# A four-layer graph network in one core: a planner that stays in a division of the array, and what is computed and loaded at the start

## The chip, the core and the metric

The kernel runs on one core of a Trainium2 chip. A core has five engines that run side by side, each with its own queue in program order: TensorE (matmuls, into PSUM), VectorE, ScalarE, GpSimd (POOL) and SyncE (SP), which here issues all DMAs. They wait for each other through semaphores. The metric is the time of one execution on the device in microseconds, as the median of several runs. The profiler's span, from the first to the last instruction, is a little shorter.

TensorE's array has 128 rows and 128 columns. It can be used whole (128\*128 in the profile), or divided: into four quarters of 64\*64, or into two halves of 128\*64. The text calls these ways of use divisions.

## The reference

All is float32. There are 128 graphs of 64 nodes with 512 features. Four layers are applied, each with a sum with its input and a layer norm over the features. Cut to what matters:

```python
# layer 0
y = x @ w;  s = y @ a
A = s[..., :, None] + s[..., None, :]
A = jnp.tanh(A / 8.0) * 8.0;  A = jnp.where(A >= 0, A, 0.1 * A)
A = jnp.exp(A) * adj;  A = A / A.sum(-1) * adj.sum(-1)      # keepdims
x = ln(x + A @ x @ w)
# layer 1
q, k, v = x @ Wq.T + bq, x @ Wk.T + bk, x @ Wv.T + bv
weight = adj * jnp.exp(q @ k.T)
x = ln(x + weight / weight.sum(2) @ v)
# layer 2
q, k = split(x @ Wqk);  v = x @ Wv
w = mask / sqrt(512) * (q * (adj @ (k * mask))).sum(-1)
x = ln(x + softmax(w)[:, :, None] * v)
# layer 3, two hypergraph convolutions; H = (adj != 0)
conv(x, W, b) = D^-1 H B^-1 H.T (x @ W.T) + b
h = ln(relu(conv(x, W1, b1)), gamma, beta)
x = ln(x + conv(h, W2, b2) + x)
```

Layer 1 needs Wq and Wk only as their product, Wq' Wk, and so does layer 2 with its two halves of Wqk. Layer 3 needs H B^-1 H' once for each graph. Its gamma can be multiplied into the rows of W2, and beta W2 is one row that is added.

## The kernel before, in words

The 8192 nodes are 64 tiles of 128 (two graphs each). A group is two tiles (GT), a chunk is two groups (GC); there are 32 groups and 16 chunks. The function `run` writes down the sixteen steps of one group, from layer 0 to the store of its output.

Large products are done by a seven-product scheme (`seven_products`): four blocks of the left side, four sums of them made on VectorE (`side_sums`), and for the weights seven pieces prepared once (`combine`), kept in DRAM and read again for every group (`streamed`, eight `ring` buffers of 512 KB). Small products per graph work in quarters: `e,x`, `gm,x` and `gm,h` (a graph's matrix times its features, in `gathered`), `e,same` (sums over a graph, `over_graph`), `ident,col`, `k,e` and `ones,e` (layer 1), and `ones,adj`, `w,kept` and `kept,kept` (a chunk's sums, and H B^-1 H'). The scores `k,k` work in column halves. All the rest takes the whole array. The profile names an instruction in this way, out<-in, by the buffers' names without numbers.

The order of all instructions on all engines is made when the program is built, by the class `Order`. Each operation is recorded by `order.add` with its engine, a cost in ns, the buffers that it reads and writes, a key (less is more urgent), and on TensorE a mode ("whole", "quarters" or "columns"). For each group `keys_by_what_follows` sets the keys from the longest chain behind an operation, between 0 and 16 steps past the group's own base (BASE). `run` of the class then plays the engines through with these costs: on each engine that is free it takes the most urgent operation that is ready and has its buffers. On TensorE, where the mode of the most urgent one differs from that of the last, an operation of the last mode is taken instead if it is within NEAR of it:

```python
if e == "SP" and heap[0][0] > far or found and heap[0][0] > found[0] + self.NEAR:
    break
```

A change of mode costs TURN ns in this play, a DMA costs 60 ns of SP and lands after its bytes have passed a link of BYTES_PER_NS, and 2200 ns. Every engine's instructions are then pinned in the order found. Since one function emits all, nearly every instruction has the same line in the profile (L1111 before).

The preparation touches these parts. `load_x`, `raw` and `load_adj` load the first group's x, the weights and the chunk's adj; w0 with its vector a0 comes first (key -11.5), x and adj after it, wq1 and wk1 at -10, wqk2 at 3. `gram` makes `m1` from wq1 and wk1, and `m2` from wqk2: four banks of four 128x512 matmuls each, copied by ScalarE. `emit_u1` makes Wk' bq by 16 matmuls of one column. `emit_bw` makes beta W2 by 16 matmuls of 128x256, and VectorE multiplies gamma into W2. `prepare_chunk` makes a chunk's H (`hA`), B^-1 (`bh`), masks and sums; H B^-1 H' (`emit_g`, buffer `gm`) is made in `run`, for each group. `normalized` does a layer norm for the two tiles of a group at once: statistics on VectorE, the power -1/2 on POOL, the scaling on ScalarE. PSUM has four buffers `bank` for single use and two pairs `chx`, `chz` for the seven products.

Of the kernel before, what the change touches and what calls it, by code (L numbers as in the profile page):

```python
# [13 lines left out]
ALU = mybir.AluOpType  # L14
# [44 lines left out]
class Order:  # L59
    LATENCY = {"PE": 220, "DVE": 70, "ACT": 60, "POOL": 60, "SP": 2200}  # L60
    BYTES_PER_NS = 230
    TURN = 100
    NEAR = 0.25
# [52 lines left out]
    def run(self):  # L116
# [5 lines left out]
        port_free, port_user = 0, None  # L122
# [5 lines left out]
        while len(done) < len(self.ops):  # L128
# [4 lines left out]
            for e, heap in ready.items():  # L133
                while free_at[e] <= now:
                    skipped, held, found = [], set(), None
                    while heap:
                        if e == "SP" and heap[0][0] > far or found and heap[0][0] > found[0] + self.NEAR:
                            break
                        item = heappop(heap)
                        need = defaultdict(int)  # L140
                        wants = [b for b in item[2].touches if b.slot is None]
                        for b in wants:
                            need[b.kind] += 1
                        if item[2].port and port_free > now:
                            skipped.append(item)
                        elif all(k not in held and len(self.slots[k]) >= c for k, c in need.items()):
                            fits = e != "PE" or item[2].mode == mode
                            if found is None or fits:
                                if found:
                                    skipped.append(found)  # L150
                                found, takes = item, wants
                            else:
                                skipped.append(item)
                            if fits or found[0] < 0:
                                break
                        else:
                            held.update(need)
                            skipped.append(item)
                    for item in skipped:
                        heappush(heap, item)  # L160
                    if found is None:
                        break
                    moved, found = True, found[2]
                    turn = 0
                    if e == "PE":
                        turn, mode = self.TURN if found.mode != mode else 0, found.mode
                    found.start = now
                    done.append(found)
                    found.takes = takes
                    for b in takes:  # L170
                        b.slot = self.slots[b.kind].pop()
                    end = free_at[e] = now + found.cost + turn
                    if found.port:
                        port_free = end
                        if e == "POOL":
                            found.behind = port_user
                        else:
                            port_user = found
                    if e == "SP":
                        link = max(link, now) + found.bytes // self.BYTES_PER_NS  # L180
                        end = max(end, link)
                    seen = end + self.LATENCY[e]
                    heappush(events, (free_at[e], n, None, None))
                    for u in found.users:
                        n += 1
                        heappush(events, (free_at[e] if u.engine == e and e != "SP" else seen, n, u, None))
                    for b in found.touches:
                        n += 1
                        heappush(events, (seen, n, None, b))
                    n += 1  # L190
# [34 lines left out]
def kernel(  # L225
# [46 lines left out]
    kind("gm", 3, GT, N)  # L272
# [29 lines left out]
    def dma(size, reads, writes, out, in_):  # L302
        order.add("SP", 60, reads, writes, lambda: nc.sync.dma_start(out=out(), in_=in_()), size=size)
# [61 lines left out]
    def raw(w, n, kind_="k4", first=()):  # L365
# [3 lines left out]
        for h in range(n):  # L369
            b = Buf(kind_, 2)  # L370
            order.add("SP", 60, [], [b, *(first if h == 0 else ())],
# [5 lines left out]
    def rows_of(b, cols):  # L377
        return b.t.rearrange("p (c o) -> p c o", o=cols)

    load_x(0)  # L380
# [4 lines left out]
        lambda: bass.AP(tensor=a0.tensor, offset=a0.offset, ap=[[0, P], [1, D]]))  # L385
    load_adj(0)
    mask_c = plain_in("mask_c", mask, T)
    order.key = -10.0
    wq1_raw, wk1_raw = raw(wq1, 2), raw(wk1, 2)
# [64 lines left out]
    def in_dram(which, width):  # L454
# [6 lines left out]
        def store(k, piece):  # L461
# [8 lines left out]
            order.add("SP", 60, [piece[0], in_turn], [dst[i % n]], emit, size=P * width * 4)  # L470
# [37 lines left out]
    def gram(name, left, right):  # L508
# [5 lines left out]
        def emit(ps, c):  # L514
            for k in range(KC):
                nc.tensor.matmul(ps.t, rows_of(left[k // 2], D)[:, k % 2, ts(c, P)], rows_of(right[k // 2], D)[:, k % 2],
                                 start=(k == 0), stop=(k == KC - 1))

        for c in range(KC):
            ps = Buf("bank")  # L520
            pe(w_pe(D, KC), left + right, [ps], lambda ps=ps, c=c: emit(ps, c))
# [11 lines left out]

    def emit_u1(ps):
        for c in range(KC):
            for k in range(KC):
                nc.tensor.matmul(ps.t[:, c : c + 1], rows_of(wk1_raw[k // 2], D)[:, k % 2, ts(c, P)], bq_c.t[:, k : k + 1],
                                 start=(k == 0), stop=(k == KC - 1))

    ps_u1 = Buf("bank")  # L540
    pe(w_pe(1, KC * KC), wk1_raw + [bq_c], [ps_u1], lambda: emit_u1(ps_u1))
# [3 lines left out]
    wqk_h = wqk2.rearrange("(h o) i -> h o i", h=2)  # L545
    order.key = 3.0
    wq2_raw, wk2_raw = raw(wqk_h[0], 2), raw(wqk_h[1], 2)
    order.key = 5.0
    m2 = gram("m2", wq2_raw, wk2_raw)

    order.key = 7.0
    stored_in_place("v2", quarter_views(raw(wv2, 2, first=[in_turn]), D), D, HALF)

    def quarters(w):
# [4 lines left out]
        for h in range(2):  # L559
            for i in range(2):  # L560
                q = Buf("k4")
                order.add("SP", 60, [in_turn] if made else [], [q] if made else [q, in_turn],
# [8 lines left out]
    order.key = 9.0  # L571
# [3 lines left out]
    ps_bw = Buf("bank")  # L575

    def emit_bw():
        for i in range(2):
            for c in range(KH):
                nc.tensor.matmul(ps_bw.t[:, ts(i, D // 2)], beta_c.t[:, c : c + 1].to_broadcast([P, P]),  # L580
                                 w3b_q[f"b{c // 4 + 1}{i + 1}"][1]()[:, c % 4, :], start=(c == 0), stop=(c == KH - 1))

    pe(w_pe(D // 2, 2 * KH), [beta_c] + [b[0] for b in w3b_q.values()], [ps_bw], emit_bw)
    act(D, [ps_bw], [bw_b], lambda: nc.scalar.activation(bw_b.t, ps_bw.t, AF.Identity, scale=0.5), NOW)
    for k, (q, view) in w3b_q.items():
        for c in range(KH // 2):
            row = (int(k[1]) - 1) * (KH // 2) + c
            dve(D // 2, [gamma_c, q], [q], lambda view=view, c=c, row=row: nc.vector.tensor_scalar(
                view()[:, c, :], view()[:, c, :], gamma_c.t[:, row : row + 1], None, ALU.mult))
    stored_in_place("3b", w3b_q, PIECE, PIECE)  # L590

    def streamed(which, room=()):
# [3 lines left out]
        for src, n in stored[which]:  # L596
            width = PIECE // src.cells
            t_ = Buf("ring")
            order.add("SP", 60, [src[list(range(n))]], [t_, *(room if not pieces else ())],
# [26 lines left out]
    def prepare_chunk(c):  # L626
        order.key = BASE[GC * c] - 3.0 if c else -9.0
# [42 lines left out]

        order.key += 6.0
# [7 lines left out]
        prepared[c] = adj, turned_adjs[c], hA, bh, am, radj, g1, dc, dh  # L679
# [164 lines left out]
    def normalized(reads_of, view, n_stats, eps, n):  # L844

        mv = Buf("col", GT)
        for t in range(GT):
# [4 lines left out]
            dve(12, [st], [mv[t]], lambda t=t, st=st: nc.vector.bn_aggr(mv.t[:, 2 * t : 2 * t + 2], st.t[:, : 6 * n_stats]), port=False)  # L852
        ve, rstd, nm = Buf("col"), Buf("col"), Buf("col")

        def pairs_of(b, i):
            return b.t[:, : 2 * GT].rearrange("p (t s) -> p t s", s=2)[:, :, i]

        dve(GT, [mv], [ve], lambda: nc.vector.tensor_scalar(ve.t[:, :GT], pairs_of(mv, 1), eps, None, ALU.add))
        order.add("POOL", 790, [ve], [rstd],
                  lambda: nc.gpsimd.tensor_tensor(rstd.t[:, :GT], ve.t[:, :GT], mhalf, ALU.pow), port=True)  # L860
        dve(GT, [mv, rstd], [nm], lambda: nc.vector.scalar_tensor_tensor(
            nm.t[:, :GT], pairs_of(mv, 0), -1.0, rstd.t[:, :GT], ALU.mult, ALU.mult))
        for t in range(GT):
            for i in range(n_stats):
                act(n // n_stats + 240, [reads_of(t, i), nm, rstd], [reads_of(t, i)], lambda t=t, i=i: nc.scalar.activation(
                    view()[:, t, ts(i, n // n_stats)], view()[:, t, ts(i, n // n_stats)], AF.Identity,
                    bias=nm.t[:, t : t + 1], scale=rstd.t[:, t : t + 1]))

    def layer_norm(xt, eps=EPS):
        normalized(lambda t, i: xt[[2 * t, 2 * t + 1]], lambda: xt.t, 1, eps, D)  # L870
# [53 lines left out]
    def run(g):  # L924
# [6 lines left out]
        adj, turned, hA, bh, am, radj, g1, dc, dh = prepared[g // GC]  # L931
# [76 lines left out]
        ps_g = Buf("bank")  # L1008

        def emit_g():  # L1010
            for t in range(GT):
                for rows, _ in halves:
                    nc.tensor.matmul(tiles(ps_g)[rows, t, :], hA.t[rows, own.start + t, :], bh.t[rows, own.start + t, :],
                                     start=True, stop=True)


# [6 lines left out]
        gm = Buf("gm")  # L1023
        pe(300, [hA, bh], [ps_g, gm], emit_g, mode="quarters")
        act(GT * N, [ps_g], [gm], lambda: nc.scalar.copy(gm.t, tiles(ps_g)), NOW)
# [26 lines left out]
        in_g = lambda h, t: gm.t[halves[h][0], t, :]  # L1052
# [34 lines left out]
        layer_norm(xt, EPS / 4)  # L1087
        order.add("SP", 60, [xt], [], lambda: nc.sync.dma_start(out=out_g[g], in_=xt.t), size=P * 4096)
# [93 lines left out]
```

## Time and profile before

| | us |
|---|---|
| median of 3 runs (2231.8 to 2235.5) | 2232.36 |
| the profiled execution | 2234.19 |
| its span | 2232.4 |
| TensorE busy (of the span) | 2202.1 (99%) |
| its weight loads | 1745.4 (78%) |
| VectorE busy | 1553.9 (70%) |
| ScalarE busy | 827.9 (37%) |
| GpSimd busy | 386.2 (17%) |
| moved by DMA | 476.44 MB, mean 213 GB/s |
| mean granted TensorE clock | 0.995 |

A line of the profile's timeline has the start and the duration in us, the engine, the line, the operation, out<-in, the shape and how many like it were merged. A float32 matmul leaves two records, so 16 matmuls are x32. The ends of matmuls are modelled: the time from one start to the next is the sharper measure. A line of the list of waits has the waiting engine and what it writes, what it waited for, the total in us, how many times, and the longest. A row of the table of stretches has the stretch, its length, the busy us of each engine, the granted clock of TensorE, the mean busy share of the 16 DMA engines and GB/s.

### The profile page before, as it was taken

What the parts mean: (1) busy time and instruction counts of PE and PEld (TensorE: products, weight loads), DVE (VectorE), ACT (ScalarE), POOL (GpSimd) and SP (SyncE); (2) the same over time, 40 slices, a digit from 0 to 9 for tenths busy, and PEclk for the clock granted to TensorE, in tenths of its full rate; (3) what the DMA queues carried; (4) which work ended last, traced back from release to release, by engine and by line L of the source; (5) the groups of instructions that cost most, each with busy time, mean ns of one, the idle gap of its engine ahead of it and who ended that gap; (6) DMA issues with size and microseconds to landing.
All of it is one profiled execution on the core that took longest, in us unless ns stands there. A gap on an engine that the chain in (4) does not pass through costs nothing.

```text
span 2232.4 us, 53041 instructions
## 1 busy us (share of the span) xinstructions
PE 2202.1 (99%) x21641; PEld 1745.4 (78%) x21641; DVE 1553.9 (70%) x4038; ACT 827.9 (37%) x1700; POOL 386.2 (17%) x398
## 2 busy tenths in 40 slices
PE   7999999999999999999999999999999999999998
PEld 4788777887878787877787878787877787878866
DVE  4676776677676777767777676777767777666675
ACT  1332443433334333334333334333334333343433
POOL 1112121121021211112121021211112211012111
PEclk9999999999999999999999999999999999999999
DMA  8566476676566666566666566666566666566475
GB/s 283 188 253 219 161 240 231 213 254 219 198 209 206 222 213 216 199 204 220 216 220 213 198 209 205 229 213 216 200 203 216 226 216 213 193 197 209 157 248 192
DMA packets 174290, 476.44 MB, mean 213 GB/s; under 512 B 35744, under 2 KB 45280, under 8 KB 174048
## 3 DMA queue, kind: packets, MB, share of 16 engines
q1 hardware_dynamic: 174048, 473.05, 63.4%
q8 instruction: 171, 2.80, 0.5%
q14 instruction: 71, 0.58, 0.1%
HBM read 443.33 MB, written 29.66 MB: 212 GB/s over the span
## 4 chain that ended last, share of the span: by engine, by line
PE 98%; DVE 1%; DMA 0%; SPq 0%; ACT 0%; issue 0%; POOLq 0%; ACTq 0%
PE bank L1111 41%; PE chx L1111 34%; PE chz L1111 23%; DVE col L1111 0%; DMA mask_c<-in_mask_dram 0%; SPq L1111 0%; DVE x L1111 0%; ACT k L1111 0%; DVE k L1111 0%; DVE e L1111 0%; ACT x L1111 0%; POOLq L1178 0%; ACTq L1178 0%; DVE h L1111 0%; ACT u_b L1111 0%
## 5 line engine op out<-in xcount | busy, mean ns | idle before, releaser
L1111 PE MATMUL chx<-ring,k 128*128 128x256 f32 (+1 forms) x1664 | 480.7, 418 | 1.5 <-DVE k L1111 1.3
L1111 ACT COPY k<-bank 128x512 f32<-128x512 f32 (+1 forms) x448 | 232.9, 558 | 523.7 <-PE bank L1111 488.2
L1111 PE MATMUL bank<-ring,k 128*128 128x256 f32 (+1 forms) x1536 | 423.2, 417 | 0.0
L1111 PEld LDWEIGHTS chx<-ring,k 128*128 128x128 f32 x1664 | 306.0, 190 | 107.5 <-issue 47.7
L1111 POOL TENSOR_TENSOR col<-col,mhalf 128x2 f32<-128x2 f32 x160 | 111.8, 699 | 1495.3 <-DVE k L1111 722.8
L1111 PEld LDWEIGHTS bank<-ring,k 128*128 128x128 f32 x1536 | 282.4, 190 | 79.2 <-issue 43.4
L1111 ACT ACTIVATE x<-x,col,col 128x512 f32<-128x512 f32 x256 | 195.8, 809 | 214.3 <-DVE col L1111 202.8
L1111 DVE SCALAR_TENSOR_TENSOR x<-chx,col,x 128x256 f32<-128x256 f32 x384 | 176.0, 479 | 105.5 <-PE chx L1111 104.2
L1111 PE MATMUL chz<-ring,h 128*128 128x256 f32 (+1 forms) x768 | 244.7, 454 | 0.2 <-DVE h L1111 0.2
L1111 PEld LDWEIGHTS chx<-k,m 128*128 128x128 f32 x1536 | 191.5, 192 | 26.1 <-issue 15.2
L1111 PE MATMUL chx<-k,m 128*128 128x128 f32 x1536 | 203.4, 275 | 0.0
L1111 PE MATMUL chz<-ring,k 128*128 128x256 f32 x768 | 202.0, 386 | 0.5 <-DVE k L1111 0.5
L1111 PEld LDWEIGHTS chz<-ring,h 128*128 128x128 f32 x768 | 140.8, 190 | 59.5 <-issue 43.9
L1111 DVE SCALAR_TENSOR_TENSOR x<-bank,col,x 128x256 f32<-128x256 f32 (+1 forms) x256 | 137.3, 547 | 66.3 <-PE bank L1111 63.9
L1111 PE MATMUL chx<-ring,h 128*128 128x256 f32 (+1 forms) x640 | 181.4, 422 | 0.0
L1111 DVE BATCH_NORM_STATS2 col<-x 128x6 f32<-128x512 f32 x256 | 175.6, 689 | 6.7
L1111 PEld LDWEIGHTS chz<-ring,k 128*128 128x128 f32 x768 | 142.4, 191 | 21.1 <-issue 2.9
L1111 ACT ACTIVATE h<-h 128x512 f32<-128x512 f32 x128 | 80.8, 632 | 208.7 <-DVE h L1111 208.5
L1111 PEld LDWEIGHTS chx<-ring,h 128*128 128x128 f32 x640 | 119.6, 190 | 31.5 <-issue 17.9
L1111 DVE SCALAR_TENSOR_TENSOR x<-chz,col,x 128x256 f32<-128x256 f32 x192 | 92.5, 482 | 65.8 <-PE chz L1111 64.4
L1111 PEld LDWEIGHTS chz<-k,m 128*128 128x128 f32 x1024 | 127.0, 192 | 12.4 <-issue 11.2
L1111 PE MATMUL chz<-k,m 128*128 128x128 f32 x1024 | 136.0, 276 | 0.0
(114 smaller groups left out, 2823.4 us busy)
## 6 DMA issues: line engine op xcount, KB each, us to landing
ring<-3a SPq DMA_DIRECT2D x224, 512.0 KB, 4.3
ring<-3b SPq DMA_DIRECT2D x224, 512.0 KB, 4.4
ring<-v SPq DMA_DIRECT2D x189, 512.0 KB, 4.3
ring<-w SPq DMA_DIRECT2D x93, 512.0 KB, 3.7
x<-in_x_dram SPq DMA_DIRECT2D x32, 512.0 KB, 4.3
out_dram<-x SPq DMA_DIRECT2D x32, 512.0 KB, 4.9
ring<-v SPq DMA_DIRECT2D x63, 256.0 KB, 3.5
ring<-w SPq DMA_DIRECT2D x31, 256.0 KB, 4.2
```

The costliest lines, as they stand in the source:

```text
L1111: made = f(*args, **kwargs)
```

## The change

The planner. TURN goes from 100 to 145, BYTES_PER_NS from 230 to 300, a DMA's cost on SP from 60 to 500, and at most eight DMAs are under way. NEAR goes from 0.25 to 0.5 and holds only while the mode is "whole"; in a divided mode the reach is FAR, 6.0. H B^-1 H' is made in `prepare_chunk`, for the four tiles of a chunk in one bank, with one copy; the buffer comes from `kept`, and `gm` is gone as a kind. wq1 and wk1 are loaded ahead of everything else (key -12), by halves in turn, w0 next, and wqk2 at -9.5. `gram` is recorded in two halves for each bank, each with its own loads. `weighted_sum` makes the sums over rows with bq and with beta on VectorE; TensorE is left with the sum over the 128 partitions, four matmuls of one column and one of 128x512. Gamma is multiplied in on ScalarE. The last group's last layer norm and store go by tile. Chunk 0 is prepared at key 0.5 instead of -9, and some keys of the preparation move.

```diff
-    BYTES_PER_NS = 230
-    TURN = 100
-    NEAR = 0.25
+    BYTES_PER_NS = 300
+    UNDERWAY = 8
+    TURN = 145
+    NEAR, FAR = 0.5, 6.0
...
-                        if e == "SP" and heap[0][0] > far or found and heap[0][0] > found[0] + self.NEAR:
+                        if e == "SP" and heap[0][0] > far or found and heap[0][0] > found[0] + (self.NEAR if mode == "whole" else self.FAR):
                             break
...
+                        landed.append(end + self.LATENCY[e])
+                        if len(landed) >= self.UNDERWAY:
+                            free_at[e] = max(free_at[e], landed[-self.UNDERWAY])
...
-        order.add("SP", 60, reads, writes, lambda: nc.sync.dma_start(out=out(), in_=in_()), size=size)
+        order.add("SP", 500, reads, writes, lambda: nc.sync.dma_start(out=out(), in_=in_()), size=size)
...
-    load_x(0)
+    order.key = -12.0
+    wq1_raw, wk1_raw = [], []
+    for h in range(2):
+        for made, w in ((wq1_raw, wq1), (wk1_raw, wk1)):
+            b = Buf("k4", 2)
+            order.add("SP", 500, [], [b], lambda b=b, h=h, w=w: nc.sync.dma_start(
+                out=rows_of(b, D), in_=w.rearrange("(h c p) o -> h p c o", h=2, p=P)[h]), size=4 * P * 1024)
+            made.append(b)
     order.key = -11.5
     w0_raw = raw(w0, 2, "ring")
...
+    load_x(0)
     load_adj(0)
...
-    wq1_raw, wk1_raw = raw(wq1, 2), raw(wk1, 2)
...
-            pe(w_pe(D, KC), left + right, [ps], lambda ps=ps, c=c: emit(ps, c))
+            for h in range(2):
+                pe(w_pe(D, KC // 2), [left[h], right[h]], [ps], lambda ps=ps, c=c, h=h: emit(ps, c, h))
...
+    def weighted_sum(columns, parts, acc, view, n):
+        for c, (b, part) in enumerate(parts):
+            if c == 0:
+                dve(n, [b, columns], [acc], lambda part=part: nc.vector.tensor_scalar(
+                    view(), part(), columns.t[:, 0:1], None, ALU.mult))
+            else:
+                dve(n, [b, columns, acc], [acc], lambda part=part, c=c: nc.vector.scalar_tensor_tensor(
+                    view(), part(), columns.t[:, c : c + 1], view(), ALU.mult, ALU.add))
+
+    acc = Buf("k2")
+    weighted_sum(bq_c, [(wk1_raw[k // 2], lambda k=k: rows_of(wk1_raw[k // 2], D)[:, k % 2]) for k in range(KC)],
+                 acc, lambda: acc.t, D)
+
     def emit_u1(ps):
         for c in range(KC):
-            for k in range(KC):
-                nc.tensor.matmul(ps.t[:, c : c + 1], rows_of(wk1_raw[k // 2], D)[:, k % 2, ts(c, P)], bq_c.t[:, k : k + 1],
-                                 start=(k == 0), stop=(k == KC - 1))
+            nc.tensor.matmul(ps.t[:, c : c + 1], acc.t[:, ts(c, P)], ones, start=True, stop=True)
...
+    order.key = -9.5
+    wq2_raw, wk2_raw = raw(wqk_h[0], 2), raw(wqk_h[1], 2)
     order.key = 3.0
-    wq2_raw, wk2_raw = raw(wqk_h[0], 2), raw(wqk_h[1], 2)
-    order.key = 5.0
     m2 = gram("m2", wq2_raw, wk2_raw)
...
-    def emit_bw():
-        for i in range(2):
-            for c in range(KH):
-                nc.tensor.matmul(ps_bw.t[:, ts(i, D // 2)], beta_c.t[:, c : c + 1].to_broadcast([P, P]),
-                                 w3b_q[f"b{c // 4 + 1}{i + 1}"][1]()[:, c % 4, :], start=(c == 0), stop=(c == KH - 1))
+    for i in range(2):
+        weighted_sum(beta_c, [(w3b_q[f"b{c // 4 + 1}{i + 1}"][0], lambda c=c, i=i: w3b_q[f"b{c // 4 + 1}{i + 1}"][1]()[:, c % 4, :])
+                              for c in range(KH)], acc_bw[i], lambda i=i: acc_bw.t[:, ts(i, D // 2)], D // 2)
+    pe(w_pe(D), [acc_bw], [ps_bw], lambda: nc.tensor.matmul(ps_bw.t, ones.to_broadcast([P, P]), acc_bw.t, start=True, stop=True))
...
-            dve(D // 2, [gamma_c, q], [q], lambda view=view, c=c, row=row: nc.vector.tensor_scalar(
-                view()[:, c, :], view()[:, c, :], gamma_c.t[:, row : row + 1], None, ALU.mult))
+            act(D // 2, [gamma_c, q], [q], lambda view=view, c=c, row=row: nc.scalar.activation(
+                view()[:, c, :], view()[:, c, :], AF.Identity, scale=gamma_c.t[:, row : row + 1]))
...
-        order.key = BASE[GC * c] - 3.0 if c else -9.0
+        order.key = BASE[GC * c] - 3.0 if c else 0.5
...
+        ps_g, gm = Buf("bank"), Buf("kept")
+
+        def emit_g():
+            for t in range(CT):
+                for rows, _ in halves:
+                    nc.tensor.matmul(ps_g.t[rows, ts(t, N)], hA.t[rows, t], bh.t[rows, t], start=True, stop=True)
+
+        pe(500, [hA, bh], [ps_g, gm], emit_g, mode="quarters")
+        act(W, [ps_g], [gm], lambda: nc.scalar.copy(flat(gm.t), ps_g.t[:, :W]), NOW)
...
-        layer_norm(xt, EPS / 4)
-        order.add("SP", 60, [xt], [], lambda: nc.sync.dma_start(out=out_g[g], in_=xt.t), size=P * 4096)
+        for among in (range(t, t + 1) for t in range(GT)) if g == NG - 1 else (range(GT),):
+            layer_norm(xt, EPS / 4, among)
+            a, b = among.start, among.stop
+            order.add("SP", 500, [xt[range(2 * a, 2 * b)]], [], lambda a=a, b=b: nc.sync.dma_start(
+                out=out_g[g][:, a:b], in_=xt.t[:, a:b]), size=P * 2048 * (b - a))
```

## The prediction

> **What bounds the kernel now.** The page comes first, then who waited for whom, then TensorE's timeline.
>
> ```profile
> span 2232.4 us, 53041 instructions
> PE 2202.1 (99%) x21641; PEld 1745.4 (78%) x21641; DVE 1553.9 (70%) x4038; ACT 827.9 (37%) x1700; POOL 386.2 (17%) x398
> ...
> PE 98%; DVE 1%; DMA 0%; SPq 0%; ACT 0%; issue 0%; POOLq 0%; ACTq 0%
> ```
>
> TensorE is busy 99% of the span and is 98% of the chain that ended last. So the span is: TensorE's first start, its work, its waits, and what follows its last matmul. From the list of waits, TensorE's own:
>
> ```profile
> PE bank L1111 <- DMA mask_c<-in_mask_dram: 11.4, 1, 11.4
> PE bank L1111 <- DVE e L1111: 3.4, 2, 2.2
> ...
> ```
>
> All its waits add to 21.9 us: 11.4 before the first instruction, 10.5 later, nearly all before 60 us. From there on it hardly ever waits, so in the steady part only TensorE time counts, and a busy TensorE can still be slow. Two things slow it. First, the divisions of the array (start, duration, then what ran; "..." joins places far apart):
>
> ```profile
> 1004.09 1.13 PE L1111 MATMUL chz<-ring,k 128*128 128x256 f32 x4
> 1005.15 1.16 PE L1111 MATMUL bank<-gm,h 64*64 64x64 f32 x64
> ...
> 1047.48 0.44 PE L1111 MATMUL bank<-e,same 64*64 64x128 f32 x4
> 1047.75 0.40 PE L1111 MATMUL bank<-ident,col 64*64 64x64 f32 x8
> 1048.08 1.16 PE L1111 MATMUL bank<-k,m 128*128 128x128 f32 x8
> ...
> 1056.07 1.03 PE L1111 MATMUL chx<-ring,k 128*128 128x256 f32 x4
> 1056.94 1.03 PE L1111 MATMUL chz<-ring,k 128*128 128x256 f32 x4
> ...
> 2076.82 0.44 PE L1111 MATMUL bank<-e,same 64*64 64x128 f32 x4
> 2077.19 1.16 PE L1111 MATMUL bank<-k,m 128*128 128x128 f32 x8
> ...
> 146.71 0.45 PE L1111 MATMUL bank<-ident,col 64*64 64x64 f32 x8
> 147.09 1.13 PE L1111 MATMUL chz<-ring,k 128*128 128x256 f32 x4
> ```
>
> Read start to start. Four whole-array records take 0.87 us among their like (1056.07 to 1056.94), 1.06 alone between two divided stretches (1004.09 to 1005.15): a whole stretch costs 0.20 us for being entered and left. A divided stretch: e,same alone 0.37 us, ident,col alone 0.38, the two in one stretch 0.60 (1047.48 to 1048.08): 0.15 us for each stretch.
>
> Second, the clock in the first 70 us (the columns after the stretch are busy us by engine; the clock stands before the DMA share):
>
> ```profile
> 40.00:50.00 10.00, 8.11 (x72) 6.56 (x65) 4.27 (x18) 1.34 (x3) 2.41 (x3) 0.67 0.64 198
> 50.00:60.00 10.00, 6.07 (x95) 4.75 (x97) 8.80 (x27) 0.78 (x4) 0.79 (x2) 0.84 0.98 371
> 60.00:70.00 10.00, 10.00 (x62) 7.50 (x60) 4.77 (x17) 3.90 (x7) 1.77 (x2) 0.65 0.29 92
> ```
>
> The loss is the busy time by one minus the clock: 0.33 x 8.1 + 0.16 x 6.1 + 0.35 x 10 = 7.2 us.
>
> **The change part by part.**
>
> *Lingering.* I counted stretches in the order in which the two built programs issue. Before: 235 whole, 209 quarter, 66 column. After: 170, 146, 63. So 65 x 0.197 + 63 x 0.147 + 3 x 0.15 (column taken as quarter) = 12.8 + 9.3 + 0.4 = **22.5 us**, all on the bounding engine. H B^-1 H' by chunk is part of it: 16 stretches' worth of kept,kept instead of 32, the same matmuls.
>
> *Sums on VectorE.*
>
> ```profile
> 35.44 3.63 PE L1111 MATMUL bank<-bq_c,k 128*128 128x1 f32 x32
> 38.99 1.42 PE L1111 MATMUL bank<-e,x 64*64 64x64 f32 x64
> ...
> 179.72 7.17 PE L1111 MATMUL bank<-k,beta_c 128*128 128x256 f32 x32
> 186.73 1.03 PE L1111 MATMUL bank<-ring,k 128*128 128x256 f32 x4
> ```
>
> Beta's 32 records took 7.0 us; one 128x512 matmul remains, two records of 0.43: **6.1 us** saved. bq's 32 took 3.55; eight of 0.11 remain: **2.65 us** saved. VectorE gets 16 x 0.48 + 4 x 0.68 = 10.4 us and gives 5.3 (gamma's 16 scalings), which ScalarE takes at about 0.37 each, 5.9 us. I cost this at nothing: around the beta sum VectorE was busy 2.7 of 10 us (180 to 190), ScalarE 37% overall. Without that cover it would be 5 us, and late next would be the row bw_b and the first use of 3b.
>
> The planner's other new constants, and the keys that move, are costed only through the order that they make.
>
> *Weights first.* On SP four 512 KB loads (0.43 to 0.49 us of issue each) now stand ahead of w0, a0, x, adj and mask, and the four of wqk2 ahead of the five vectors, the seven stores of w0, wv1, x1 and the second adj. In the trace the second 512 KB load was used at 5.77 us, so the first gram product can start near **5.8 us** instead of the 11.4 of the first instruction and the 18.3 of the gram now. The windows moved 264 GB/s in 0 to 20 us and 316 in 20 to 40, so 5.3 MB by 20 us and 11.6 by 40. 6.3 MB stand up to wqk2's last piece: about 23 us. TensorE comes to it at 24 (m1's 32 records of 0.43, u0 0.9, adj's sums 1, and the cold start), so no wait. But wv1 ends at 10.2 MB, 35.6 us (used at 30.4 now), and the second adj at 10.9, about 37.6. VectorE's queue has three sums over wv1 ahead of group 0's side sums, so those are late by the wv1 load, and TensorE behind them: 1.5 us. Then the chain of groups 0 and 1 through VectorE (some 9 us of its work to group 1's e) with the second gram already spent as filler: I put 5 us of idling there.
>
> What TensorE loses at the start now: 21.9 waits + 7.2 clock + 2.3 cold (the first eight gram records took 5.77 us, later ones 3.44) = 31.4. After: 5.8 + 2.3 + 1.5 + 5 + 3.5 (one dip of the clock after the thin stretch) = 18.1. Gain **13.3 us**. Bounds: 4 (the thin stretch as long as now and a second dip) to 20 (no thin stretch).
>
> The rule that bears on this is the Trainium skill's "TensorE: Matmul & The Clock Gate" (Why this matters for your kernels): no idle gaps over about 3 us between bursts, else half rate. It speaks against the change, since the filler is gone where group 1 waits. But the row disagrees with it on the first dip: the clock fell near 40 us with no gap over 0.7 us before it; what stood there were 3.6 us of 128x1 matmuls. By the row the dip goes with bq's matmuls, by the rule it has another cause and may stay: 2.7 us less gain. I go by the row.
>
> *The end.*
>
> ```profile
> 2227.03 1.52 ACT L1111 ACTIVATE x<-x,col,col 128x512 f32<-128x512 f32 x2 [11.19 <-DVE col L1111]
> 2228.57 0.39 SPq L1111 DMA_DIRECT2D out_dram<-x  x1
> ```
>
> The last group is normalised and stored by tile: one ScalarE pass instead of two before the last store (0.7 us) and half the bytes behind it. But the first tile's last small VectorE step is issued behind the second tile's statistics, so its pass isn't early: **1.2 us** (0.5 to 1.5).
>
> *New waits.* No row shows them. From below nothing; from above about 12 us: in ten long quarter stretches kept,kept and ident,col write banks that ScalarE has just to empty (0.59 us a copy, two copies, 1.1 us of other matmuls between), so 0.6 us each if ScalarE is late, and some 0.2 us a group elsewhere since TensorE runs ahead of the plan. Nearest is the trace, where such orders wait almost never: **3 us**.
>
> *Sum.* 22.5 + 6.1 + 2.65 + 13.3 + 1.2 - 3 = 42.7. The profiled execution took 2234.2 (span 2232.4, 1.8 around it), 1.8 over the median of the runs: 2191.5 for it, **2190** for the median.
>
> **The rivals.**
> *The start gives little.* 476 MB are moved, and from 10 to 40 us the DMA share is near 1: loads put first push others back by what they bring. If the gain is 2 instead of 13: 2201. Against it: the second gram's 13.7 us ran in the busy part (67 and 88 us) and now fill time in which TensorE idled.
> *New waits take half of the switches.* A stretch of six kinds stands in order, and the first unready one holds all. 11 us more: 2201, to 2213 with the upper bound.
> *More than that.* No thin stretch, no dip, no new waits: 2180.
> *Slower.* Only four banks: a divided operation taken up to six steps early holds a bank until ScalarE has copied it (0.59 us), and the next whole product waits. It decides from 45.7 us (the gains without the 3), 1.4 us in each of 32 groups, or nearly two and a half such copies waited out in full; three of them (57 us) end at 2244. Against it: ScalarE is busy 37%, and now every group waits about nothing.
>
> **How the numbers follow.** Likeliest 0.52 (2182 to 2199); little at the start 0.20; new waits 0.15; more 0.09; slower, or no difference, 0.04. The range 2176 to 2211 leaves out the far ends of the waits, the far end of "more" and the slower case. 0.2% (4.5 us) is about what a measurement of this kernel can tell from no change. Faster 0.95, same 0.015, slower 0.035.
>
> **What would show it.** Right: 130 fewer divided and whole stretches with the same 0.20 and 0.15; TensorE busy near 2170 us, first matmul near 6 us, a list of TensorE's waits below 20 us; a clock row without the dip at 40 us; beta's row gone. Wrong: TensorE waits of over 10 us after 60 us on ScalarE or VectorE (then the order is at fault), waits on wv1, adj or x landings at 35 to 40 us (then the loads), or a busy TensorE that hasn't fallen, which would mean that the price of a stretch isn't paid per stretch.

## The result, and the profile after

The changed kernel takes 2194.49 us (median of 4 runs, 2192.11 to 2194.97) against 2232.34 beside it: a ratio of 0.9825 (95% interval 0.9808 to 0.9842), 37.9 us less. Forecast were 2190 and a range of 2176 to 2211. The profiled execution took 2194.68 us, its span is 2192.8.

The page of the kernel after, its first lines; then the list of TensorE's waits:

```profile
span 2192.8 us, 52900 instructions
PE 2166.0 (99%) x21587; PEld 1744.5 (80%) x21587; DVE 1562.4 (71%) x4044; ACT 823.2 (38%) x1700; POOL 385.7 (18%) x399
```

```profile
PE bank L1134 <- DMA k<-in_wk_dram: 6.3, 1, 6.3
PE bank L1134 <- issue: 6.1, 4, 2.9
PE bank L1134 <- DVE e L1134: 3.7, 2, 2.0
PE chx L1134 <- issue: 2.0, 3, 1.2
...
PE bank L1134 <- ACT k L1134: 0.3, 1, 0.3
```

TensorE is busy 36.1 us less. Its first matmul stands at 6.25 us instead of 11.41. What has grown is the releaser "issue", which stands for no releaser at all: 8.2 us in seven waits, called unnamed waits from here on. A line of this kind was in the list before as well, and I had passed over it (the kernel before):

```profile
PE bank L1111 <- issue: 1.6, 2, 1.1
```

Stretches of the array's divisions, counted in the trace, are 170 whole, 146 quarter and 63 column, as in the built order. Beta's 32 records are two, and bq's 32 are eight of 1.0 us together. The table of stretches after (columns as in the prediction):

```profile
40.00:50.00 10.00, 10.00 (x79) 6.89 (x77) 6.67 (x25) 1.60 (x7) 2.74 (x4) 1.00 0.94 315
50.00:60.00 10.00, 6.32 (x116) 4.83 (x116) 8.36 (x24) 3.59 (x7) 2.34 (x4) 0.83 0.95 329
60.00:70.00 10.00, 10.00 (x56) 8.70 (x55) 4.43 (x14) 2.44 (x8) 2.17 (x2) 0.66 0.41 130
```

The dip of the clock at 40 us is gone; the one that follows group 1's thin stretch, where TensorE waits twice for VectorE, has stayed, at 56 us:

```profile
53.75 0.44 PE L1134 MATMUL bank<-e,same 64*64 64x128 f32 x4 [1.96 <-DVE e L1134]
55.90 1.51 PE L1134 MATMUL bank<-e,x 64*64 64x64 f32 x64 [1.71 <-DVE e L1134]
```

The largest of the seven unnamed waits, in the timeline:

```profile
346.60 1.15 PE L1134 MATMUL bank<-k,k 128*64 128x64 f32 x32
347.68 1.04 PE L1134 MATMUL bank<-kept,h 64*64 64x64 f32 x55
351.58 0.35 PE L1134 MATMUL bank<-kept,h 64*64 64x64 f32 x9 [2.86 <-issue]
```

TensorE stops for 2.86 us inside one operation, between two matmuls that read the same buffers and write the same bank: nothing in the program stands between them.

### The profile page after: what moved, and what is told of

It reads as the page before. It is cut to its first block, busy times and chain, and to the rows that moved or that the text cites. A ratio compares the mean times of both kernels' runs of the same rounds, so it can differ in the third digit from the quotient of the medians.

```text
span 2192.8 us, 52900 instructions
## 1 busy us (share of the span) xinstructions
PE 2166.0 (99%) x21587; PEld 1744.5 (80%) x21587; DVE 1562.4 (71%) x4044; ACT 823.2 (38%) x1700; POOL 385.7 (18%) x399
## 4 chain that ended last, share of the span: by engine, by line
PE 97%; DMA 1%; DVE 1%; issue 0%; ACT 0%; SPq 0%; DVEq 0%; ACTq 0%
PE bank L1134 40%; PE chx L1134 35%; PE chz L1134 23%; DMA x<-in_x_dram 0%; DMA out_dram<-x 0%; DMA k<-in_wk_dram 0%; DVE col L1134 0%; DVE x L1134 0%; ACT k L1134 0%; DVE h L1134 0%; ACT x L1134 0%; DVE e L1134 0%; DVE k L1134 0%; SPq L1134 0%; DVE m L1134 0%
## 5 line engine op out<-in xcount | busy, mean ns | idle before, releaser
L1134 POOL TENSOR_TENSOR col<-col,mhalf 128x2 f32<-128x2 f32 (+1 forms) x161 | 111.5, 693 | 1481.1 <-DVE col L1134 910.7
L1134 ACT COPY k<-bank 128x512 f32<-128x512 f32 (+1 forms) x448 | 226.4, 560 | 343.9 <-PE bank L1134 330.4
```

The source lines that it names most:

```text
L1134: made = f(*args, **kwargs)
```

## Where the time goes, in one account

From a trace the time up to the last matmul can be split: first start, waits, half of the time at half clock (which the clock's records give), and what is left, TensorE's work at full clock. "By price" is the prediction's price (0.197, 0.147 and 0.15 us a stretch, and 8.75 us for the sums where they are on VectorE) against the kernel before; all in us. The waits of this table count every gap, also the short ones that the list of waits leaves out. The other kernels in it are runs of the next section.

| kernel | stretches | work, by price | work, measured | unnamed waits after 110 us | other waits after 110 us | lost to clock dips after 110 us |
|---|---|---|---|---|---|---|
| before | 235/209/66 | 0 | 0 | 1.6 | 1.4 | 0 |
| after | 170/146/63 | -31.3 | -32.7 | 8.2 | 1.6 | 0 |
| e1_no_linger | 197/182/63 | -20.7 | -19.3 | 22.1 | 4.6 | 6.8 |
| e2_short_reach | 217/186/66 | -15.7 | -16.7 | 0.7 | 5.2 | 0 |
| e3_old_loads | 164/140/59 | -33.9 | -32.3 | 13.4 | 3.7 | 6.8 |
| e4_tensor_sums | 167/140/62 | -24.1 | -22.5 | 14.2 | 2.9 | 5.1 |
| e5_linger_alone | 167/139/61 | -24.4 | -25.9 | 9.2 | 3.5 | 3.4 |

The price of a stretch holds within 2 us of the sum in six kernels. What differs beside it is the column of unnamed waits, and the dips of the clock that some of them bring.

## The experiments

**The linger, the reach, the loads and the sums, one at a time.** These four ran first, before the unnamed waits were understood.

```diff
-    NEAR, FAR = 0.5, 6.0
+    NEAR, FAR = 0.5, 0.5
```

> The changed kernel with the reach in a divided mode set back to that of the whole mode (0.5 and 0.5). Its order has 197 whole, 182 quarter and 63 column stretches, against 170, 146 and 63. Theory A (each stretch has its price, 0.197 us a whole one, 0.147 a quarter one): 27 x 0.197 + 36 x 0.147 = 10.6 us slower than the changed kernel's 2194.5, 2205; if the unnamed waits of the changed kernel (8.2 us in all after 110 us, against 1.6 before) come with the longer quarter stretches, up to 5 us of that come back: 2200 to 2206. Rival B (the gain is of the start and of the order as such, the count of stretches is immaterial): within 4 us of 2194.5.

Measured: 2228.89 us, ratio to before 0.9981 (0.9971 to 0.9991). Far above both expectations. Its waits:

```profile
PE bank L1134 <- issue: 22.1, 9, 3.0
...
PE bank L1134 <- ACT k L1134: 4.2, 12, 0.4
```

22.1 us of unnamed waits, nine of 1.1 to 3.0 us, and four dips of the clock of 3.4 us: 14 + 7 us over the kernel after in the profiled run, with 3 more of named waits and 13 for the stretches that come back.

```diff
-    TURN = 145
-
-    NEAR, FAR = 0.5, 6.0
+    TURN = 100
+
+    NEAR, FAR = 0.25, 0.25
```

> The changed kernel with the planner's reach as before in both modes (0.25) and its price of a turn as before (100). 217 whole, 186 quarter, 66 column stretches. Theory A: 47 x 0.197 + 40 x 0.147 + 3 x 0.15 = 15.6 us slower than 2194.5, 2210, or 2205 if 5 us of waits go. A second point for the price of a stretch. Rival B: within 4 us of 2194.5.

Measured: 2205.59 us, 0.9877 (0.9863 to 0.9892). It has 20 whole stretches more than the run before and is 23 us faster:

```profile
PE bank L1134 <- ACT k L1134: 3.4, 13, 0.7
...
PE bank L1134 <- issue: 0.6, 1, 0.6
```

So the number of stretches alone doesn't set the time. The third puts the load order of the kernel before back (`load_x(0)` first, wq1 and wk1 at key -10, wqk2 at 3); the fourth puts the sums with bq and beta back on TensorE and gamma on VectorE, by the removed lines of the diff.

> The changed kernel with the loads in the old order: x, w0, a0, adj first, wq1 and wk1 after them, wqk2 at key 3. 164 whole, 140 quarter and 59 column stretches, 2.7 us fewer than in the changed kernel by their price. Theory A (the start is worth 13 to 14 us): 2194.5 + 14 - 2.7 = 2206, TensorE's first instruction near 11 us. Rival (the start gives little, the filler is only moved): 2192 to 2197.

Measured: 2211.53 us, 0.9901 (0.9885 to 0.9918), 5.5 over the expectation. Its profiled span is 19.1 us over that of the kernel after; 5.2 of them are unnamed waits, 6.8 late dips of the clock and 2.1 other late waits. At the start it loses 4.8 us of first start (11.04) and 1.4 of waits, and 1.7 less to a dip: the loads by themselves are worth 4.5 us.

> The changed kernel with both sums over rows on TensorE again (32 records of 128x1 for bq, 32 of 128x256 for beta) and gamma on VectorE again. 167 whole, 140 quarter and 62 column stretches, 1.6 us fewer by their price. Theory A: 2194.5 + 8.75 - 1.6 = 2201.6. On the clock: if the dip near 40 us before came from the 128x1 matmuls, a dip of some 7 us follows them here too; by the rule of idle gaps there is none. Rival (VectorE's 10 us of sums delay the chain as much as TensorE gains): within 3 us of 2194.5.

Measured: 2215.85 us, 0.9925 (0.991 to 0.9939), 14 over. Unnamed waits 6.0 and dips 5.1 more than after. It also answers a question of the prediction. bq's matmuls in the timeline, and the clock just behind them in the table of stretches:

```profile
23.54 3.63 PE L1136 MATMUL bank<-bq_c,k 128*128 128x1 f32 x32
```

```profile
26.00:28.00 2.00, 2.00 (x43) 1.99 (x42) 1.42 (x4) 0.08 (x1) 0.86 (x1) 1.00 1.04 342
28.00:30.00 2.00, 2.00 (x33) 1.59 (x30) 1.36 (x10) 0.81 (x3) 0.99 (x2) 0.60 1.03 335
30.00:32.00 2.00, 2.00 (x4) 0.79 (x3) 0.24 (x1) 0.00 (x0) 0.61 (x1) 0.54 0.84 245
```

TensorE was busy without a break, and the clock fell.

**What the unnamed waits are.** The page's list of DMA queues has one, q8, of kind "instruction" (packets, MB, share of the 16 engines' time):

```profile
q8 instruction: 171, 2.80, 0.5%
```

These are 16.4 KB for each packet. TensorE's records are 43,838 (21,587 matmuls, as many weight loads, and 664 of its sequencer), 256 for each packet. I numbered them in the order of the trace. At every unnamed wait of over 0.3 us after 110 us, in every kernel, the first record behind the wait has a number that leaves 193 when divided by 256. So TensorE's instructions come in blocks of 256, and the wait is at a block's edge. Three times tell the rest, measured from the edge before to the wait's end (us):

```
                        256 records   next packet starts   TensorE resumes
                        ran in        after the edge       after that start
after     at  351.58    2.69          3.48                 2.28
after     at  576.02    2.25          1.99                 2.33
after     at 1375.70    2.30          0.92                 2.31
e1        at  579.8     2.20          3.01                 2.44
e1        at 1259.4     2.68          3.55                 2.31
```

There is one packet for each edge. With the weights' full traffic it starts 0.4 to 4.5 us behind the edge at these waits, and TensorE goes on 2.2 to 2.8 us after its start (3.1 and 3.2 us in two cases): the packet that starts behind one edge is needed at the next, so no more than one block is ahead. Where the whole block is of the whole-array mode, 256 records run for 18 to 25 us and nothing shows. Where 64x64 matmuls are dense they run in 2.0 to 4 us, and TensorE can be through before the next block is there. It isn't always: of the seven blocks after 110 us that the changed kernel ran in under 2.8 us, four ended in an unnamed wait; in front of the other three the packet had started 0.1 us behind the edge at the latest, or ahead of it. The Trainium skill, "Runtime: NRT & Kernel Launch" (Instruction fetch mechanics), has the same blocks of 256 instructions, but says that crossing an edge is "mostly hidden"; for these stretches the trace disagrees, with up to 3.6 us for one edge.

Three runs test this theory, F. The first sets the planner's new reach and TURN alone into the kernel before:

```diff
-    TURN = 100
-    NEAR = 0.25
+    TURN = 145
+    NEAR, FAR = 0.5, 6.0
...
-... found[0] + self.NEAR:
+... found[0] + (self.NEAR if mode == "whole" else self.FAR):
```

> The kernel before with NEAR, FAR = 0.5, 6 and TURN 145 alone: 167 whole, 139 quarter, 61 column stretches instead of 235, 209, 66. Price per stretch: 68 x 0.197 + 70 x 0.147 + 5 x 0.15 = 24.4 us, so 2208.7 less what is lost to new waits. Theory F (TensorE's instructions come in blocks of 256 over a DMA queue, one block ahead, and a block of divided matmuls that runs in under 3 us is over before the next has landed): 5 to 15 us of waits without a named releaser after 110 us, each at a block's edge, so 2213 to 2223. Theory P (the price alone): 2208 to 2210, with waits as before, 3 us.

Measured: 2222.4 us, 0.9954 (0.9939 to 0.9968): at the upper end for F, 12 over the price alone. Five unnamed waits, 9.2 us, and two dips. So about half of the linger's 24.4 us is given back when it stands alone.

The second moves the block edges and nothing else:

```diff
+    for _ in range(36):
+        nc.tensor.matmul(kinds["bank"][3][:N, :1], same[:N, :N], ones[:N], start=True, stop=True)
     order.keys_by_what_follows()
```

> The changed kernel with 36 matmuls of one column (144 instructions) ahead of the first load's arrival; the order behind them is the same. Theory F: the seven unnamed waits (351.6, 576.0, 778.2, 1177.3, 1375.7, 1577.3, 1775.1 us) are gone from their places; new ones stand where the shifted block edges follow a block run in under 3 us: near 242, 263, 352 (another matmul), 442, 507, 844, 909, 1242, 1308, 1642, 1707 and 1842 us, though not at all of them; 10 to 25 us together instead of 8.2, so 2196 to 2213. Theory B (the waits belong to these matmuls: a bank that ScalarE has to empty, a semaphore): the same seven places with the same 8 us, 2194 to 2195.

Measured: 2213.35 us, 0.9912 (0.9896 to 0.9928), 18.9 over the kernel after, the upper end for F. Same place in its timeline:

```profile
347.98 1.16 PE L1134 MATMUL bank<-kept,h 64*64 64x64 f32 x64
348.96 0.87 PE L1134 MATMUL bank<-e,x 64*64 64x64 f32 x47
352.80 0.50 PE L1134 MATMUL bank<-e,x 64*64 64x64 f32 x17 [2.97 <-issue]
```

The kept,h that stood apart by 2.86 us now runs through, and the wait is in e,x: with 144 records more ahead, the edges come 144 records earlier in the order, and so the next one 112 later, which are the 9 matmul records of kept,h and the 47 of e,x with their weight loads. All seven waits have left their places. Eleven of the twelve named places have one (at their times in the shifted run, up to 22 us later: 242, 353, 446, 515, 855, 923, 1260, 1326, 1661, 1729 and 1864 us), one (263) has none, and 797.8 has one that I hadn't named (its 256 records ran in 3.95 us). Together 21.0 us, and five dips, 8.5 us. The theory that the waits belong to banks, semaphores or ScalarE falls.

The third takes away what a packet may have to wait behind:

```diff
-                          out=t_.t[:, : n * width], in_=src.t[:, : n * width]),
+                          out=t_.t[:, : n * width // 8], in_=src.t[:, : n * width // 8]),
```

> The changed kernel with only the first eighth of each weight piece read again from DRAM for each group (seven eighths of that traffic left out, so the products use stale pieces); the same instructions on every engine. Theory F with the fetch waiting behind data packets: the unnamed waits after 110 us fall from 8.2 us to under 2, 2186 to 2189. If a fetch takes as long without the traffic: they stay at 6 to 9 us, 2193 to 2195.

Measured: 2181.92 us, 0.9775 (0.976 to 0.9789), 12.6 under the kernel after. The same kept,h, and the list of waits:

```profile
343.01 1.14 PE L1134 MATMUL bank<-kept,h 64*64 64x64 f32 x59
344.34 0.33 PE L1134 MATMUL bank<-kept,h 64*64 64x64 f32 x5 [0.19 <-issue]
```

```profile
PE bank L1134 <- issue: 1.7, 4, 0.6
```

At these waits the packets now start 0.25 to 0.5 us after the edge, and TensorE resumes 2.3 to 2.7 us after that as ever: the delay comes with the weights' traffic, the rest belongs to the fetch. The edges don't all stand where they were, since TensorE has 80 semaphore records fewer here; but as many blocks run in under 2.8 us (eight against seven), so the waits didn't shrink for want of dense blocks. 6.5 us of unnamed waits and 0.9 of others go, and the dip at 56 us is 3.4 us long instead of 10.2, another 3.4 us; some 1.8 us are not accounted for by waits and dips (by the book of the table TensorE's work is 2.2 us less). The floor is seen too: a block that ran in 2.0 us still waits 0.4.

**The rest of the start.** e7 moves the last bank of the second gram to where TensorE waits for group 1's e; in e9 its two ScalarE copies stand ahead of the bank's next use and its three sums later. (In e7 the copies came behind that use, so a part of m2 held other values; the number of instructions is the same.) The edit, in the order that the planner found:

```diff
+    planned.insert(planned.index(at_same), first)
+    planned.insert(planned.index(at_e_x), second)
...
+    planned[i:i] = copies
...
+    planned[i:i] = sums
```

> The changed kernel with the last bank of the second gram (two pairs of 128x512 matmuls, 3.6 us) moved from 44 to 48 us to just ahead of group 1's e,same and e,x, where TensorE waits 1.96 and 1.71 us. If the dip of the clock at 56 us comes with the thin stretch: no waits there and no dip, 3.7 + 4.5 = 8 us less, 2186 to 2187. If the dip comes with the quarter matmuls, whatever stands between: 3.7 less, 2191. If VectorE's chain sets the end of the start: the waits come back at the next operation of the chain, 2193 to 2195.

Measured: 2191.73 us, 0.9811 (0.9795 to 0.9828). No wait at e,same or e,x over 0.25 us and no dip at 56 us, as the first case had it; but 1.8 us of wait came back at a later product behind VectorE, and two unnamed waits (2.96 and 2.12 us) brought dips of 6.8 and 3.4 us.

> The edit of the run before that moved the gram, with its two ScalarE copies now ahead of the bank's next use and its three sums later on VectorE. TensorE's waits before 110 us fall from 3.7 us after the first load to under 2, the dip at 56 us (10.2 us at half clock, 5.1 lost) is gone: 5 to 8 us less than the changed kernel if the unnamed waits at block edges keep their 8 us, so 2186 to 2190; up to 5 us of that is lost again if two of these waits bring a dip of the clock of their own (2191 to 2192).

> The changed kernel once more beside it, for the comparison: 2194 to 2195, with the seven unnamed waits at the same instructions, 7 to 9 us together.

Measured side by side: 2189.47 us, 0.9809 (0.9796 to 0.9823), against 2193.76 and 0.983 (0.9817 to 0.9844) for the unchanged one. The timeline of e9:

```profile
48.71 1.88 PE L1138 MATMUL bank<-k,k 128*128 128x512 f32 x4
50.84 0.44 PE L1138 MATMUL bank<-e,same 64*64 64x128 f32 x4 [0.25 <-DVE e L1138]
51.21 1.98 PE L1138 MATMUL bank<-k,k 128*128 128x512 f32 x4
53.12 1.16 PE L1138 MATMUL bank<-e,x 64*64 64x64 f32 x64
```

The clock stays at 1.00 from 50 to 68 us. The time is inside 2186 to 2190. The gain over the repeated kernel is 4.3 us by the medians and 5.3 by the profiled spans (2191.8 and 2186.5), at or just under the lower end of the 5 to 8 us expected, and the two intervals just overlap. It is the fastest kernel here that computes everything. The repeated one has its unnamed waits at five of the seven places of before, of 0.4 to 3.6 us: the places belong to the order, the lengths to the run. In line with that, kernels with many such waits spread (2209 to 2217 us in e6), while the kernel before stays within 2230 to 2234 in the same run.

## Why the prediction was right, and where it was not

The time was within 4.5 us of the forecast and inside the range. The mechanism of the largest term is right; one term, the new waits, was sized wrong and its cause not seen. That the place of the block edges kept it small is luck, as e6 shows.

*Lingering and sums.* 131 stretches fewer, as counted. Predicted 22.5 + 8.75 = 31.3 us, measured 32.7 less TensorE work. Right. ScalarE and VectorE took gamma and the sums without a wait that shows.

*The start.* In the prediction's terms: first start 6.25 (5.8 put), cold start 3.0 (2.3), waits 3.7, both for group 1's e (1.5 + 5 put), the dip 4.5 (3.5): 17.4 against 18.1. The second gram fills what had been idle, as argued; the wait behind wv1's load didn't come. The 31.4 that I set against it held 3.0 us of waits after 110 us, though the prediction has nearly all of the later waits before 60 us; so the start itself gained 11.0 by this book, not 13.3. And I had put it down to the loads: with the old order of loads (e3) 4.5 of it are lost. The rest is not lost with the sums or the reach put back: first start, waits and dips up to 110 us add to 27.3 us before and 15.1 after, to 13.6 with the sums back on TensorE (e4), to 14.7 and 14.5 with a shorter reach (e1, e2). The linger set into the kernel before (e5) leaves them at 27.6. What else was changed there, such as the later preparation of chunk 0 or the grams in halves, no run takes apart, so the greater part of this gain has no shown cause.

*The dip at 40 us.* By the row it goes with bq's matmuls, by the rule it could stay. It went; and with bq's matmuls back (e4) a dip is there with no idle time before it. The second dip is nearer to the rule, but not to its 3 us: two gaps of 1.96 and 1.71 us with 0.4 us of work between were enough, and with both filled (e9) it is gone. What the traces show in place of the 3 us stands at the end of this section.

*The end.* 1.2 us forecast; from the last matmul's end to the end of the span it was 8.49 us and is 7.13: 1.36. In the timeline after, the first tile's pass is the one that still comes late:

```profile
2188.17 1.58 ACT L1134 ACTIVATE x<-x,col,col 128x512 f32<-128x512 f32 x2 [12.45 <-DVE col L1134]
2189.01 1.10 SPq L1134 DMA_DIRECT2D out_dram<-x  x2
```

The two passes stand back to back behind VectorE's columns, and the first store can only start between them.

*New waits.* This is the step that failed: "Nearest is the trace, where such orders wait almost never: 3 us", and the bound above it by banks that ScalarE has just to empty. Waits after 110 us went from 3.0 to 9.8 us, 6.8 more, and of the 9.8 ScalarE's banks have 0.3. The 6.6 us more of unnamed ones are instruction fetches that dense divided stretches outrun, which the prediction did not name. Had the changed order met the edges as e6 does, the time would have been 2213, outside the range: that it met them better was not planned.

*The rivals.* "The start gives little" falls by the first start and the row at 40 us. "New waits take half" had a size near the truth (7 of 11 us) with a cause that the runs refute. "More than that", 2180, needs no new waits: e8 comes to 2181.92 by leaving out traffic. "Slower" by held banks: 0.3 us of it here, and at most 4.2 us in twelve waits (e1) in any run.

Account of the 39.6 us of span: 32.7 work, 5.2 first start, 3.7 waits and 3.4 dips (by the clock's records) at the start, 1.4 end, minus 6.8 new waits: 39.6.

When an unnamed wait brings a dip of the clock can be read from the twelve traces, though no run was made to test it. In each trace the clock's records begin and end on a grid of 3.41 us, and the dips before the last matmul are one, two or three steps of it. From the first clock record on and at full clock, TensorE was idle for 1.83 us or more in 31 of these steps, and half clock followed every one; of 98 steps with 0.4 to 1.77 us of idle time it followed two. In those two, and in the two steps without idle time that half clock followed (at 40 us before, at 28 us in e4), stand 0.9 to 3.0 us of matmuls of one or two columns; these seem to count much like idle time, though one step with 1.95 us of them (e5, at 31 us) was not followed by a dip. So what counts is how the grid cuts a wait. The 2.86 us of the changed kernel were cut into 1.36 and 1.50, and no dip came. In its repetition e10 the wait at the same place was 3.62 us, cut into 1.08 and 2.54:

```profile
351.68 0.35 PE L1134 MATMUL bank<-kept,h 64*64 64x64 f32 x9 [3.62 <-issue]
```

The row behind the wait, in the kernel after and then in e10:

```profile
352.00:354.00 2.00, 2.00 (x68) 1.82 (x58) 0.84 (x3) 1.98 (x5) 0.00 (x0) 1.00 0.61 234
352.00:354.00 2.00, 2.00 (x70) 1.79 (x62) 0.76 (x2) 1.79 (x4) 0.00 (x0) 0.64 0.38 142
```

The grid stands elsewhere in every run, so this too is luck. Open is whether the edges have a better place: no run looked for it. The order repeats every three groups, in nearly 16 blocks, so a shift that helps one place may hurt another.

## What to carry to other kernels

Order by count of stretches saves what the price says, but look at the density as well: where TensorE runs 256 instructions in less than some 4 us (here 64 float32 matmuls of 64x64), the next block may be late, and later with the weights' traffic than without it (e8). A wait "issue" inside one operation, which moves when a few instructions are put ahead, is the sign; and two versions of such a kernel that differ by a few early instructions (36 matmuls in e6) can differ by 19 us for that reason alone, so compare their waits before their times.

## What the runs showed of the hardware that was not expected

TensorE's instructions arrive in packets of 256, and data traffic holds these packets up: at the unnamed waits a packet starts 0.25 to 0.5 us after the edge with an eighth of the weights' traffic and up to 4.5 us after it with all of it, and from its start to the first new matmul it is mostly 2.2 to 2.8 us. A dip of the clock followed where TensorE was idle for 1.83 us or more of one 3.41 us step, and hardly ever below that. A dip lasts 3.41 us or a small multiple of it, and costs half of that.
